# The dense products of layer 3 of a four-layer transformer moved behind the routed experts

## The chip, the cores and the metric

The kernel runs on one core of a Trainium2 chip. The core has a matrix engine (TensorE; its matmuls are PE in the profile, its weight loads PEld), a vector engine (VectorE, DVE), a scalar engine (ScalarE, ACT), a general engine (GpSimd, POOL) and a queue engine that issues plain DMAs (SyncE, SP). Each engine works through its own list of instructions, and engines wait for each other by semaphores. The metric is the device time of one execution in microseconds; the number given is the median of several runs.

## The reference

Four layers work on `x`, 4 rows of 1024 tokens with 128 features. Each layer is a token mixer and a feed-forward part, and after each of the two comes `x = layernorm(x + f(x))`. The change touches the feed-forward part of the last layer, a mixture of experts with a dense "shared" part beside it:

```python
logits = flat.astype(jnp.float32) @ router_w.T + router_bias
scores = jax.nn.softmax(logits, axis=-1)
topk_scores, topk_idx = jax.lax.top_k(scores, TOPK)          # 4 of 32 experts
topk_scores = topk_scores / jnp.clip(topk_scores.sum(axis=-1, keepdims=True), 1e-12, None)
h = jax.nn.silu(jnp.einsum('nd,ehd->neh', flat, gate_w)) * jnp.einsum('nd,ehd->neh', flat, up_w)
expert_out = jnp.einsum('neh,edh->ned', h, down_w)
sel = jnp.take_along_axis(expert_out, topk_idx[:, :, None], axis=1)
out = (sel * topk_scores.astype(flat.dtype)[:, :, None]).sum(axis=1)
out = out + jax.nn.silu(flat @ sgate_w.T) * (flat @ sup_w.T) @ sdown_w.T
```

The last line is the shared part: 128 features up to 512, a gate, and down again, for every token. All sums are in float32.

## The kernel before

`x` stays on the chip as 32 tiles of 128 tokens; a turned copy `xT` feeds the products. For layer 3 the tokens are cut by position into three parts: `a` (the first half of each row, 16 tiles), `b` and `c` (a quarter each, 8 tiles). For each part the work is a chain.

- `l3_attn` (L1621) is the mixer: a norm (BATCH_NORM on VectorE, `rstd` on ScalarE), `sq`, turned into `xq`, products `s`, on VectorE the `y` and `u` chain (L1694 to L1700), products back, a norm, and the turned `xT`.
- `l3_route` (L1718) is the router: softmax, the four largest, and in `positions` a place for each (token, expert) pair in a list sorted by expert. It writes `pos` (L1302).
- `spread` (L1373) scatters the rows of `x` into that list in DRAM (`l3ra`, `l3rb`, `l3rc`) by indirect DMAs that POOL issues, four for a tile: 64 for part a, 32 for b and 32 for c.
- `l3_experts` (`small_experts`, L1781) goes over the list in groups of four tiles: 20 groups for a, 12 each for b and c. For a group, SP loads the rows (`xg`, L1392), PE turns them (`tp`, to `xgT`), multiplies by the gate and up weights (`gu`), ScalarE and VectorE make `sg` and `hg`, PE turns that (`hT`, L173) and multiplies by the down weights (`yp`), ScalarE copies it out (`yg`), and SP writes it to `l3ya`, `l3yb` or `l3yc` (L1830). After the last group `rest_of` (L1414) has a branch (L1418, L1419) over groups that a list has only when it is unusually long.
- `collect` (L1441) gathers each token's four results back (`yt`, again indirect DMAs of POOL, four for a tile, L1327) and adds them to `x` on VectorE with their weights (L1452). The pool of `yt` has eight buffers, taken in turn by all tiles of all parts.
- `finish` (L1866), or `close` (L1946) for part c, norms `x` and writes the output.

The shared part is `l3_shared` (L1749): a block is four tiles. For each of four chunks of 128 hidden features it makes two products of 512 columns (`pg`, `pu`), `sg` on ScalarE and `hs` on VectorE (L764), then 16 products down (`py`). Part a has four blocks, b and c two each.

The order of the work is planned when the program is built. A stage is a main generator and a side generator: `mix(main, side, pace)` runs the main one and, for each unit of planned time that it reports, lets the side report 1/pace units. `press` runs only the side until a condition holds. The side of this stage is called `on`: it holds the mixers and routers of b and c, the scatters of b and c, and the gathers and norms of a and then b. A scheduler then places the instructions on each engine, in an order that is fixed in the built program. What the main generators are, in order:

1. `l3_shared(a)`, then `l3_experts(a)`, at pace 0.45;
2. for b: `l3_shared(b)` as soon as b's mixer is through, its result kept in `sh` by ScalarE copies (L1769), since b's rows are not yet scattered; then `l3_experts(b)`, in whose end (`held`, L1739) `sh` is added to `x`;
3. for c: the same, and `on` is drained inside the end of `l3_experts(c)`;
4. `close(c)`: c's gathers, two tiles for a row, its norm and output.

Of the kernel before, what the change touches and what calls it, by code (L numbers as in the profile page):

```python
# [30 lines left out]
QT = NT // NQT  # L31
# [11 lines left out]
E3, F3, K3 = 32, 128, 4  # L43
# [31 lines left out]
class Kernel:  # L75
# [677 lines left out]

    def glu(self, ps, hp, dst, wg, wu, blk):

        nc = self.nc
        c = slice(blk * BLK, (blk + 1) * BLK)
        pg = self.tile(ps, [P, BLK], "pg")
        self.mm(pg, wg, self.xT[:, c])
        pu = self.tile(ps, [P, BLK], "pu")  # L760
# [3 lines left out]
        nc.vector.tensor_tensor(dst, sg, pu, ALU.mult)  # L764

    def down(self, ps, h, wd, nch):

        py = self.tile(ps, [P, 4, D], "py")
# [969 lines left out]

    def held(self, part, sh):  # L1739

        s = slice(part.t0, part.t0 + part.nt)
        self.nc.vector.tensor_tensor(self.x[:, s, :], sh, self.x[:, s, :], ALU.add)
        yield (1.0,)

    def mark(self, name):
        self.listed.add(name)
        yield (0.0,)

    def l3_shared(self, part, sw, sh=None):  # L1749

        nc, x = self.nc, self.x
        NC = FS3 // P
        with ExitStack() as c2:
            hp = self.pool(c2, "l3sh" + part.name, 2)
            ps = self.pool(c2, "l3sp" + part.name, 2, space=PSUM)
            assert sh is not None or "l3" + part.name in self.listed
            wd = sw[:, 2, :].rearrange("p (c d) -> p c d", d=D)
            for blk in range(part.t0 // 4, (part.t0 + part.nt) // 4):
                h = self.tile(hp, [P, NC, BLK], "hs", bufs=1)
                for c in range(NC):  # L1760
                    f = slice(c * P, (c + 1) * P)
                    self.glu(ps, hp, h[:, c, :], sw[:, 0, f], sw[:, 1, f], blk)
                py = self.down(ps, h, wd, NC)
                if sh is None:
                    s = slice(blk * 4, blk * 4 + 4)
                    nc.vector.tensor_tensor(x[:, s, :], py, x[:, s, :], ALU.add)
                else:
                    t = blk * 4 - part.t0
                    nc.scalar.copy(sh[:, t : t + 4, :], py)  # L1769
                yield (9.0,)  # L1770
# [10 lines left out]
    def small_experts(self, lay, ne, part, wall, held=None):  # L1781

        nc = self.nc
# [3 lines left out]
        with ExitStack() as ctx:  # L1787
# [57 lines left out]
            for g in range(ng + 1):  # L1845
# [7 lines left out]
                if g == ng:  # L1853
                    while held and (got := self.queued(held)):
                        self.now += got[0]
                    self.rest_of(used, tl, total, rest)
                    self.listed.add(f"made {lay}{part.name}")
# [31 lines left out]
    def at_once(self, gen):  # L1889

        for _ in gen:
            yield (0.0,)

    def served(self, gen, *others):
# [46 lines left out]

    def last(self, part, yp):
        yield from self.collect("l3", part, K3, yp)
        yield from self.finish(part)

# [11 lines left out]
    def all(self):  # L1957
# [4 lines left out]
        with ExitStack() as ctx:  # L1962
# [37 lines left out]
            with ExitStack() as c3:  # L2000
                with ExitStack() as c2:
# [12 lines left out]
                    self.abreast(  # L2014
                        self.chain(self.l3_attn(b), self.mark("mixed l3b"), self.l3_route(b)),
                        self.collect("l2", n2, K2, yp, which=(2, 3, 6, 7)),
                    ),
                    self.abreast(
                        self.chain(
                            self.spread("l3", b, K3), self.when(listed("made l3a")), self.last(a, yp),  # L2020
                        ),
                        self.chain(
                            self.l3_attn(c), self.mark("mixed l3c"), self.l3_route(c),
                            self.at_once(self.spread("l3", c, K3)),
                        ),
                    ),
# [12 lines left out]
                self.run(self.close(c, yp))  # L2039
# [183 lines left out]
```

## Time and profile before

| what | value |
|---|---|
| runs (us) | 1927.78, 1932.83, 1929.3; median 1929.3 |
| profiled execution (us) | 1937.33, span 1935.5 |
| PE busy | 1541.5 us, 80% of the span |
| VectorE busy | 1199.2 us, 62% |
| ScalarE busy | 900.6 us, 47% |
| POOL busy | 690.3 us, 36% |
| mean granted PE clock | 0.896 |

The span is the time from the first to the last instruction; the execution is a little longer. The profile gives busy time for each engine, 40 slices of the span with the busy tenths in each, groups of like instructions with what ended the idle time before them, and the instructions in order of time. A share over the whole span says little here: the change touches only the last fifth, from 1549.7 us on, so the stages there are read one by one.

In the last fifth, part a's shared products run from 1549.7 to 1596, its experts to 1708, part b's shared products (with quarter c's routing beside them) to 1743, b's experts to 1793.5, part c's shared products to 1816, c's experts to 1866.5, and the closing work to 1935.5.

### The profile page before, as it was taken

How to read it: one execution, taken by the hardware profiler on the slowest of the kernel's cores; microseconds unless marked ns; L12 is line 12 of the kernel's file. 1: busy time of each engine (PE TensorE's matmuls, PEld its weight loads, DVE VectorE, ACT ScalarE, POOL GpSimd, SP SyncE). 2: the span in 40 equal slices, each digit the busy share in tenths (PEclk: the TensorE clock that was granted, in tenths of full speed). 3: DMA queues.
4: the chain of work that ended last, by engine and by line, in shares of the span. 5: the costliest groups of instructions: out<-in, count | busy, mean ns of one | idle time of the engine just before them, and what ended most of it. 6: DMA issues, size and time to landing. Idle time of an engine off the chain costs nothing. (4 is left out here: it accounts for less than half of the span.)

```text
span 1935.5 us, 27095 instructions
## 1 busy us (share of the span) xinstructions
PE 1541.5 (80%) x9025; PEld 920.8 (48%) x9025; DVE 1199.2 (62%) x3491; ACT 900.6 (47%) x1349; POOL 690.3 (36%) x670
## 2 busy tenths in 40 slices
PE   7885677597847887989977878798798998999850
PEld 3332433385423345856632232333355757768650
DVE  8998698465766664635564565546442446866383
ACT  5876265243324554423336756564532236644330
POOL 2000148604630660265443000030536430567775
PEclk9897688798978998999988988898988999989985
DMA  9990002244430113632241000000452213425452
GB/s 297 288 288 10 1 17 86 87 126 133 159 129 18 60 63 129 183 96 73 78 137 32 1 1 1 2 23 1 159 213 83 66 28 93 141 68 167 122 147 61
DMA packets 215530, 187.10 MB, mean 97 GB/s; under 512 B 16528, under 2 KB 194064, under 8 KB 214864
## 3 DMA queue, kind: packets, MB, share of 16 engines
q1 hardware_dynamic: 194672, 142.29, 23.6%
q0 software_dynamic: 20704, 42.86, 7.3%
q8 instruction: 84, 1.38, 0.3%
q14 instruction: 70, 0.57, 0.1%
HBM read 88.49 MB, written 96.60 MB: 96 GB/s over the span
## 5 line engine op out<-in xcount | busy, mean ns | idle before, releaser
L1081 ACT ACTIVATE pr<-sc 128x1024 f32<-128x1024 f32 x288 | 279.4, 1021 | 175.2 <-PE sc L161 174.8
L161 PE MATMUL sc<-qm,kT 32*128 32x512 f32 (+3 forms) x1536 | 197.7, 559 | 16.7 <-ACT pr L1081 16.7
L161 PE MATMUL s<-pr,va 128*32 128x512 f32 (+3 forms) x1536 | 167.5, 532 | 19.0 <-DVE x L1019 10.2
L161 PE MATMUL gu<-ld,xgT 128*128 x640 | 165.1, 400 | 10.2 <-DVE hg L1812 5.9
L1087 DVE TENSOR_TENSOR pr<-pr,ld 128x512 f32<-128x512 f32 (+1 forms) x160 | 91.7, 581 | 105.6 <-ACT pr L1081 105.4
L161 PE MATMUL gu<-wall,xgT 128*128 x304 | 148.2, 612 | 2.0 <-ACT xgT L171 2.0
L161 PEld LDWEIGHTS sc<-qm,kT 32*128 32x128 f32 x1536 | 83.7, 194 | 112.4 <-issue 61.1
L161 PEld LDWEIGHTS gu<-ld,xgT 128*128 128x128 f32 x640 | 119.5, 198 | 34.7 <-DVE hg L1812 6.1
L1812 DVE TENSOR_TENSOR hg<-sg,gu 128x256 f32<-128x256 f32 x160 | 66.0, 417 | 92.0 <-ACT sg L1811 91.6
L173 DVE COPY hT<-tp 128x512 f32<-128x512 f32 x118 | 80.9, 686 | 66.2 <-PE tp L169 66.2
L1567 ACT ACTIVATE sg<-gu 128x512 f32<-128x512 f32 x76 | 45.4, 597 | 144.7 <-PE gu L161 143.6
L1811 ACT ACTIVATE sg<-gu 128x256 f32<-128x256 f32 x160 | 61.3, 385 | 107.7 <-PE gu L161 79.8
L171 ACT COPY xgT<-tp 128x512 f32<-128x512 f32 x99 | 58.0, 586 | 99.9 <-PE tp L169 99.8
L1327 POOL DMA_INDIRECT l1ra<-x,posl1a x64 | 79.8, 1246 | 61.3 <-DVE peq L1321 42.0
L1327 POOL DMA_INDIRECT l1rr<-x,posl1r x64 | 65.4, 1022 | 100.9 <-DVE posl1r L1302 70.8
L169 PEld LDWEIGHTS tp<-ld,hg 128*128 128x128 f32 x624 | 77.4, 141 | 49.0 <-issue 32.5
L1569 DVE TENSOR_TENSOR hg<-sg,gu 128x512 f32<-128x512 f32 x76 | 51.8, 682 | 78.9 <-ACT sg L1567 78.8
L1327 POOL DMA_INDIRECT l2rm<-x,posl2m x16 | 15.7, 983 | 236.8 <-DVE peq L1320 230.1
L169 PE MATMUL tp<-ld,hg 128*128 128x128 f32 x624 | 96.4, 275 | 3.7 <-DVE hg L1812 2.0
L1327 POOL DMA_INDIRECT l3ra<-x,posl3a x64 | 63.7, 996 | 93.3 <-DVE usedl3a L1315 51.0
L161 PEld LDWEIGHTS s<-pr,va 128*32 128x32 f32 x1536 | 37.1, 113 | 122.6 <-issue 78.4
L161 PE MATMUL yp<-ld,hT 128*128 x640 | 86.1, 276 | 2.3 <-DVE mv L197 1.5
(447 smaller groups left out, 3439.1 us busy)
## 6 DMA issues: line engine op xcount, KB each, us to landing
wall<-wall SPq DMA_DIRECT2D x16, 768.0 KB, 7.8
l3ra<-zero SPq DMA_DIRECT2D x1, 6144.0 KB, 25.5
ld<-in_l_w SPq DMA_DIRECT2D x2, 3072.0 KB, 10.6
wall<-we SPq DMA_DIRECT2D x24, 256.0 KB, 2.1
ld<-in_l_w SPq DMA_DIRECT2D x1, 6144.0 KB, 20.6
l1ra<-zero SPq DMA_DIRECT2D x1, 5120.0 KB, 19.6
l1rr<-zero SPq DMA_DIRECT2D x1, 5120.0 KB, 23.1
xg<-l3ra SPq DMA_DIRECT2D x20, 256.0 KB, 2.9
```

The source lines that it names most:

```text
L161: return self.nc.tensor.matmul(out, lhsT, rhs, start=start, stop=stop)
L169: nc.tensor.transpose(pt[:, k * P : (k + 1) * P], s, self.ident)
L171: nc.scalar.copy(dst, pt[:, : n * P])
L173: nc.vector.tensor_copy(dst, pt[:, : n * P])
L1081: nc.scalar.activation(pr, sc[h], AF.Exp)
L1087: nc.vector.tensor_tensor(d, d, cst["tril"].unsqueeze(1).unsqueeze(1).to_broadcast([P, 2, n, P]), ALU.mult)
L1327: ins = self.nc.gpsimd.indirect_dma_start(**kw)
L1567: nc.scalar.activation(sg, gu[:, 0, :], AF.Silu)
L1569: nc.vector.tensor_tensor(h, sg, gu[:, 1, :], ALU.mult)
L1811: nc.scalar.activation(sg, pg[:, :, 0, :], AF.Silu)
L1812: nc.vector.tensor_tensor(h[:, 2 * c : 2 * c + 2, :], sg, pg[:, :, 1, :], ALU.mult)
```

## The change

Part a's experts come first, and its shared products behind them. Parts b and c then run only their experts. Their shared products, b's two blocks and c's two, come behind the last groups of c's experts, within the same pools of PSUM and ahead of the branch of `rest_of`; what is left of `on` is drained beside them. No result is held back in `sh`: every block is added to `x` at once from PSUM by VectorE, since all rows have been scattered by then. The norms of a and b wait (in the plan) until their shared products are in. The mixer and router of b count 0.6 of their planned time, so that more of them is planned beside the same main work.

```diff
-    def l3_shared(self, part, sw, sh=None):
+    def l3_shared(self, part, sw, ps=None):
...
-            ps = self.pool(c2, "l3sp" + part.name, 2, space=PSUM)
-            assert sh is not None or "l3" + part.name in self.listed
+            ps = ps or self.pool(c2, "l3sp" + part.name, 2, space=PSUM)
+            assert "l3" + part.name in self.listed
...
-                    self.glu(ps, hp, h[:, c, :], sw[:, 0, f], sw[:, 1, f], blk)
-                py = self.down(ps, h, wd, NC)
-                if sh is None:
-                    s = slice(blk * 4, blk * 4 + 4)
-                    nc.vector.tensor_tensor(x[:, s, :], py, x[:, s, :], ALU.add)
-                else:
-                    t = blk * 4 - part.t0
-                    nc.scalar.copy(sh[:, t : t + 4, :], py)
+                    self.glu(ps, hp, h[:, c, :], sw[:, 0, f], sw[:, 1, f], blk, ("tp", "gu"))
+                py = self.down(ps, h, wd, NC, "yp")
+                s = slice(blk * 4, blk * 4 + 4)
+                nc.vector.tensor_tensor(x[:, s, :], py, x[:, s, :], ALU.add)
                 yield (9.0,)
...
                 if g == ng:
-                    while held and (got := self.queued(held)):
+                    for got in held(ps) if held else ():
                         self.now += got[0]
                     self.rest_of(used, tl, total, rest)
...
+    def scaled(self, gen, by):
+
+        for got in gen:
+            yield (got[0] * by, *got[1:])
...
-    def last(self, part, yp):
+    def last(self, part, yp, ready=lambda: True):
         yield from self.collect("l3", part, K3, yp)
+        yield from self.when(ready)
         yield from self.finish(part)
...
-                        self.chain(self.l3_attn(b), self.mark("mixed l3b"), self.l3_route(b)),
+                        self.scaled(self.chain(self.l3_attn(b), self.l3_route(b)), 0.6),
...
-                            self.spread("l3", b, K3), self.when(listed("made l3a")), self.last(a, yp),
+                            self.spread("l3", b, K3), self.when(listed("made l3a")), self.last(a, yp, listed("shared l3a")),
...
-                            self.l3_attn(c), self.mark("mixed l3c"), self.l3_route(c),
+                            self.l3_attn(c), self.l3_route(c),
...
-                    self.when(listed("made l3b")), self.last(b, yp),
+                    self.when(listed("made l3b")), self.last(b, yp, listed("shared l3b")),
                 )
-                self.run(self.mix(self.chain(self.l3_shared(a, sw), self.l3_experts(a, wall3)), on, 0.45, False))
-                hold = self.pool(c3, "l3hold", 2)
-                for p in (b, c):
-                    self.press(on, listed("mixed l3" + p.name))
-                    sh = self.tile(hold, [P, QT, D], "sh")
-                    self.run(self.mix(self.l3_shared(p, sw, sh), on, 0.75, False))
-                    self.press(on, listed("l3" + p.name))
-                    self.press(on, listed("mixed l3c"))
-                    ahead = self.chain(self.held(p, sh), on) if p is c else self.held(p, sh)
-                    self.run(self.mix(self.l3_experts(p, wall3, ahead), on, 0.75, False))
+                self.run(self.mix(self.l3_experts(a, wall3), on, 0.45, False))
+                self.run(self.mix(self.chain(self.l3_shared(a, sw), self.mark("shared l3a")), on, 0.45, False))
+                self.press(on, listed("l3b"))
+                self.run(self.mix(self.l3_experts(b, wall3), on, 0.75, False))
+                self.press(on, listed("l3c"))
+                rest = lambda ps: self.mix(
+                    self.chain(self.l3_shared(b, sw, ps), self.mark("shared l3b"), self.l3_shared(c, sw, ps)), on, 0.75
+                )
+                self.run(self.mix(self.l3_experts(c, wall3, rest), on, 0.75, False))
                 self.run(self.close(c, yp))
```

`glu` and `down` take the names of the PSUM tiles to use, so that the shared products of b and c can use the experts' tiles `tp`, `gu` and `yp`.

More of the change, by code (lines that the diff above doesn't have):

```diff
@@ L751, in weigh, with glu @@
         nc.vector.tensor_tensor(w, w, red.unsqueeze(2).to_broadcast([P, nt, ne]), ALU.mult)
-    def glu(self, ps, hp, dst, wg, wu, blk):
+    def glu(self, ps, hp, dst, wg, wu, blk, tags=("pg", "pu")):
         nc = self.nc
         c = slice(blk * BLK, (blk + 1) * BLK)
-        pg = self.tile(ps, [P, BLK], "pg")
+        pg = self.tile(ps, [P, BLK], tags[0])
         self.mm(pg, wg, self.xT[:, c])
-        pu = self.tile(ps, [P, BLK], "pu")
+        pu = self.tile(ps, [P, BLK], tags[1])
         self.mm(pu, wu, self.xT[:, c])
@@ L764, in glu, with down @@
         nc.vector.tensor_tensor(dst, sg, pu, ALU.mult)
-    def down(self, ps, h, wd, nch):
-        py = self.tile(ps, [P, 4, D], "py")
+    def down(self, ps, h, wd, nch, tag="py"):
+        py = self.tile(ps, [P, 4, D], tag)
         for k in range(4):
@@ L1737, in l3_route @@
             yield (10.0,)
[L1739 to L1743, printed above, removed]
     def mark(self, name):
```

## The prediction

> **What bounds the kernel now.** I read the page's 40 slices first, then the busy time by stage, then the instructions in order of time on SP, VectorE (DVE) and GpSimd (POOL) at the seams between stages. The change lies wholly behind 1549.7 us, where layer 2's last experts end. POOL's slices:
>
> ```profile
> POOL 2000148604630660265443000030536430567775
> PEclk9897688798978998999988988898988999989985
> ```
>
> From slice 36 on POOL shows 6 to 7 tenths; in 10 us slices it is 7.56 us of 10 from 1713 to 1920, one indirect DMA every 1.26 us without a hole. So now the tail is POOL's: 64 gathers of list a, 32 scatters of list c, 32 gathers of b, 32 of c are 160 x 1.26 = 202 us, measured 1712.8 to 1921.2. The engines by stage (columns: stretch, its length, then busy us of PE, PEld, DVE, ACT, POOL, and PE's granted clock):
>
> ```profile
> 1549.70:1596.00 46.30, 43.25 (x201) 27.40 (x202) 20.61 (x52) 16.27 (x30) 15.14 (x16) 1.00 0.11 29
> 1596.00:1657.00 61.00, 55.18 (x328) 44.91 (x328) 45.85 (x168) 35.48 (x68) 0.00 (x0) 0.97 0.33 96
> 1657.00:1708.00 51.00, 46.14 (x288) 37.90 (x286) 40.91 (x126) 31.34 (x61) 35.01 (x32) 1.00 0.45 137
> 1708.00:1743.00 35.00, 32.06 (x127) 20.13 (x125) 20.10 (x81) 15.74 (x25) 23.18 (x24) 0.80 0.20 52
> 1743.00:1793.50 50.50, 45.45 (x291) 40.60 (x289) 30.94 (x76) 23.91 (x49) 38.43 (x40) 0.97 0.57 168
> 1793.50:1816.00 22.50, 21.62 (x96) 13.24 (x96) 5.41 (x8) 5.60 (x10) 17.10 (x18) 1.00 0.27 73
> 1816.00:1866.50 50.50, 45.41 (x288) 40.53 (x288) 27.99 (x73) 23.67 (x49) 37.01 (x39) 0.97 0.63 167
> 1866.50:1877.60 11.10, 0.00 (x0) 0.00 (x0) 10.96 (x55) 1.88 (x3) 7.62 (x9) 0.68 0.58 151
> ```
>
> These are: shared a; experts a up to list b's positions; the rest of experts a; shared b with quarter c's routing; experts b; shared c; experts c; then VectorE alone. PE is busy 289 of 317 us up to 1866.5: barely less full than POOL. The two chains end within 11 us of each other, so whichever the change lengthens decides. Their meeting point:
>
> ```profile
> 1875.33 0.98 POOL L1327 DMA_INDIRECT yt<-l3yb,posl3b  x1 [0.30 <-issue]
> 1877.59 3.44 POOL L1327 DMA_INDIRECT yt<-l3yc,posl3c  x1 [1.28 <-DVE x L1452]
> ```
>
> The first gather of c waited for VectorE's adds of b (L1452), because gathers use eight buffers in turn: c's first tile takes the buffer of b's first. From that gather to the end of the span it is 1935.5 - 1877.6 = 57.9 us, 32 gathers at POOL's pace, the last adds, norm and write: the same in both kernels.
>
> **The change, part by part.** The work is the same but for small things: four ScalarE copies of `sh` (0.59 us each) and two VectorE adds (1.22 us) go, two more block adds of 0.69 us come; no DMA is added, and POOL's order of gathers and scatters stays. Each costs nothing on the path by itself. The extra condition in `last` emits no instruction. What counts is the order, taken from the built program's instruction streams, into which I put the durations of the rows.
>
> (1) Experts a now start the stage, with nothing beside their start. SP may not load their rows until the branch is passed, which waits for the last writes to land. Rows (start us, length, engine, line, operation; in brackets the idle time ahead and what ended it):
>
> ```profile
> 1743.12 15.13 SPq L1392 DMA_DIRECT2D xg<-l3rb  x7
> ...
> 1754.24 0.68 DVE L173 COPY hT<-tp 128x512 f32<-128x512 f32 x1
> ...
> 1761.33 0.68 DVE L173 COPY hT<-tp 128x512 f32<-128x512 f32 x1
> 1764.87 0.68 DVE L173 COPY hT<-tp 128x512 f32<-128x512 f32 x1
> ...
> 1797.68 1.28 DVE L764 TENSOR_TENSOR hs<-sg,pu 128x512 f32<-128x512 f32 x2 [5.18 <-SPq L1419]
> ```
>
> SP released VectorE 4.0 us after the last `l3yb` write was issued (1793.7). The last layer 2 write is issued at 1549.4, so the first load goes out at about 1553. From first load to first `hT` done it is 1754.9 - 1743.1 = 11.8 us, then 1764.87 - 1761.33 = 3.55 us a group. The order puts quarter b's norm behind the fifth `hT`: 1553 + 11.8 + 14.2 = 1579, with its adds 1580. Before, it began at 1584.0: 4 us gained for 42 us of products moved out of the way.
>
> (2) Quarter b's chain, norm to list positions, took 1656.6 - 1584.0 = 72.6 us beside nine groups; now also nine, without four shared products on VectorE (4 x 0.69): 69.5, so 1649.5. From there to the end of experts a it took 51.4 us; five groups fewer remain (5 x 3.55 = 17.8), but quarter c's chain is the same and VectorE, busy 40.9 of 51, gets denser: I add 3. End of experts a: 1686, 22 us earlier. Bounds of (1) and (2): 1675 (loads at 1550, no loss by density) to 1695.
>
> (3) Shared a behind them: four blocks at 10.44 us (their block adds L1766 come at 1561.2, 1571.7, 1582.1) and 1.2 to start, 43 us. Quarter c's norm and routing now run inside. Before, they cost 35 - 22 = 13 us beyond two blocks, part of it at half clock (0.80 mean). By the new order block 2's products wait for the norm and both `xT` copies. I take 12, nearest that row; bounds 4 and 14. End 1741.
>
> (4) Experts b: 50.5 us as before, 1791.5. Then experts c directly: no shared product stands between, so the 4 us of SP's branch, which shared c used to cover, is bare, and so is their start. 1791.5 + 4.3 + 50.5 = 1846. Bounds of the 4.3: 0 and 5.2.
>
> (5) Shared b and c: four blocks, 42 us, to 1888 if undisturbed. But VectorE's order has, ahead of block 3's products, eight adds of the last two tiles of a (2.8 us) and both norms of half a, which before ran in the stretch 1866.5 to 1877.6 with PE idle anyway: 32 statistics (about 7 us), two scalings of eight (2.16 each). In a strict order these are 14 us ahead of block 3's second and third product, of which some 3 are covered by PE's two buffers: 11 us. Bounds 3 (nearly all hidden) and 14; a gain is excluded, since these instructions now only stand ahead of products. End of shared c's last add: 1899.
>
> (6) In VectorE's order all 32 adds of b stand behind that last add. After four of them (1.4) and 1.3 us, as in the row of 1877.59, c's first gather goes at 1902, against 1877.6. Sum +24. The queue behind this wait on POOL is all of c's 32 gathers, and behind them the output.
>
> The Trainium skill, "TensorE: Matmul & The Clock Gate" (section on the array's architecture, engine queue depths), calls VectorE's and ScalarE's queues strict FIFOs. The trace agrees as far as it goes: the add at 1867.86 and the norms came before any add of b, though b's tiles had landed. By the rule the sum stays at +24; if VectorE could pass over the waiting shared products, c's gathers would start when POOL is free, and the sum would be -18.
>
> The same page (Part 1) has PE fall to half clock after about 3.4 us idle and return after as long at work. Here the clock is 0.50 from 1748 to 1751 after 3.4 us idle, inside the 11.8 us used above; but from 1711 to 1723 it stayed at 0.50 with PE at work, longer than the page says, so a measured ramp is used instead of the rule.
>
> The profiled execution took 1937.33 us, 1.8 around its span, and 8.0 above the median 1929.3 of the runs. The sum is a difference inside it; I apply it to the median: 1929.3 + 24 = 1953.
>
> **Rivals.** (a) POOL still sets the end, faster. Positions of b come at 1649.5, its scatters take 44.5 us (measured 1657.5 to 1702.0), and list a is written at 1686 + 3: a's gathers start at about 1695 instead of 1712.8, -18: 1911. For it: POOL has no holes before. Against it: c's first gather needs VectorE through shared c by 1871, and my sum is 28 us past that. That one point decides.
> (b) The seams fill: shared a costs 4 beyond its blocks, the norms cost 3, the bare branch 0: 8 + 8 + 4.3 less, +4, 1933. For it: PE's products need few of VectorE's instructions in shared b and c. Against: each low bound must hold at once.
> (c) PE cools in the new holes, at 1549, 1792 and in block 3, as it did from 1711 to 1723 for 12 us at half clock (6 us lost): twice that, +36, 1965.
>
> **How the numbers follow.** The main case 0.80, (a) 0.06, (b) 0.06, (c) 0.08. A measurement here tells about 0.3%, 6 us, from no change; (a) is faster; (b) lies within it, as does little of the main case; (c) and the rest are slower: 0.06, 0.07, 0.87. Low bounds of (1) to (5) together take off 11 + 8 + 4 + 8, which reaches no change, high ones add 15; a part of each gives 1935 to 1967.
>
> **What would show it.** Right: first load of a's rows at 1552 to 1554; experts a over at 1680 to 1692; a hole of 7 us or more on PE between experts b and c; a's norms within shared c's first block with PE waiting for VectorE; POOL idle for 15 us or more ahead of c's first gather, released by VectorE; PE's last product past 1885. Wrong: POOL without a hole to the end, or shared c's last add before 1875. What would break it most easily is step (2): VectorE packs the chain closer than the rows show, and everything after it moves up.

## The result, and the profile after

The changed kernel took 1935.28 us (median of 20 runs, 1928.87 to 1941.33); the kernel before took 1929.87 us beside it (20 runs). The ratio is 1.0023, 95% interval 1.0012 to 1.0034: slower by 0.23%, some 4 us (the medians differ by 5.4), which is inside the 0.3% that the text had set as no change. The prediction was 1953.0 us, slower by 24; it gave 0.07 to "same". The direction was right and the size was wrong by a factor of five. The time lies 0.3 us inside the low end of the range, which says little for the working: experts a ended earlier than the low bound of steps (1) and (2) allows, as shown below. Some chips run every kernel here about 17% longer (2245 to 2274 us for the kernel before); runs from those are named, and only their ratios to the kernel before on the same chip and the order of their events are read.

Both kernels are the same up to the issue of layer 2's last write, and that instant drifts: it stood at 1549.4 us in the profiled execution before, at 1541.0 in the one after, and between 1540.5 and 1548.0 in the seven other kernels that ran at this speed. So from here on times are counted from it, written with a plus sign: before, the span ends at 1935.5 - 1549.4 = +386.1; after, at 1933.4 - 1541.0 = +392.4. The stretch that the change touches grew by 6.3 us, though the profiled span after is the shorter one.

POOL's 40 slices of the kernel after (48.3 us each):

```profile
POOL 2000147514630660265443000031536321777545
```

POOL is at 7 tenths earlier than before, in slices 35 to 37 (1643 to 1788 us), and then falls to 5 and 4 where the kernel before stood at 7. The engines by stage, as for the kernel before (columns: stretch, its length, busy us of PE, PEld, DVE, ACT, POOL, then PE's granted clock):

```profile
1541.04:1666.50 125.46, 108.35 (x612) 87.98 (x612) 90.21 (x303) 71.43 (x140) 42.34 (x42) 0.93 0.38 111
1666.50:1715.30 48.80, 47.97 (x231) 31.18 (x231) 31.65 (x118) 19.08 (x32) 37.22 (x39) 1.00 0.20 53
1715.30:1765.35 50.05, 46.12 (x288) 41.46 (x288) 29.18 (x72) 22.68 (x47) 38.15 (x40) 0.93 0.54 167
1765.35:1821.45 56.10, 46.41 (x292) 41.46 (x292) 23.80 (x56) 23.85 (x49) 38.04 (x41) 0.91 0.60 162
1821.45:1871.03 49.58, 44.69 (x190) 27.35 (x189) 24.97 (x83) 13.99 (x21) 16.09 (x18) 0.93 0.22 57
```

These are experts a; shared a with route c inside; experts b; the bare branch and experts c; shared b and c. The first stretch is cut at the branch behind experts a; the last product of experts a ends at 1662.74, and quarter c's own products follow up to the branch. Shared a is the surprise: 48.0 of 48.8 us busy, at full clock, although most of quarter c's routing stands in it. The rows that answer to those of the prediction, from the instructions in order of time (start, length, engine, line, operation; in brackets the idle time ahead and what ended it):

```profile
1541.62 15.90 SPq L1392 DMA_DIRECT2D xg<-l3ra  x7
1545.21 1.09 PE L169 MATMUL tp<-ld,xg 128*128 128x128 f32 x4 [4.92 <-DMA xg<-l3ra]
1630.73 0.15 DVE L1302 TENSOR_SCALAR posl3b<-pm 128x32 uint32<-128x32 f32 x1
1774.21 2.29 PE L169 MATMUL tp<-ld,xg 128*128 128x128 f32 x8 [8.86 <-DMA xg<-l3rc]
1850.01 1.70 PE L161 MATMUL gu<-xT,ld 128*128 128x512 f32 x2 [3.39 <-DVE hs L764]
1870.34 0.69 DVE L1759 TENSOR_TENSOR x<-yp,x 128x512 f32<-128x512 f32 x1 [3.26 <-PE yp L161]
1873.37 7.11 POOL L1327 DMA_INDIRECT yt<-l3yc,posl3c  x1 [18.51 <-DVE x L1452]
```

What the reader is to see: list b's positions come at +89.7 (before +107.2); PE idles 8.9 us at the branch behind experts b; it waits for VectorE inside shared c's first block; and POOL stands 18.5 us until VectorE has shared c's last add (1870.34) and the first adds of b behind it. So the place that the prediction named is where the end is decided. Only, it comes 20 us earlier than predicted: c's first gather goes at +332.3, where the text had 1902 - 1549.4 = +352.6, and the kernel before +328.2.

### The profile page after: what moved, and what is told of

Read it like the earlier page. It is cut to its first block, busy times and chain, and to the rows that moved or that the text cites. A ratio compares the mean times of both kernels' runs of the same rounds, so it can differ in the third digit from the quotient of the medians.

```text
span 1933.4 us, 27089 instructions
## 1 busy us (share of the span) xinstructions
PE 1538.2 (80%) x9025; PEld 924.7 (48%) x9025; DVE 1198.5 (62%) x3493; ACT 897.1 (46%) x1346; POOL 692.1 (36%) x670
## 5 line engine op out<-in xcount | busy, mean ns | idle before, releaser
L161 PE MATMUL gu<-ld,xgT 128*128 x640 | 168.6, 407 | 11.2 <-ACT rms L1657 4.4
L1327 POOL DMA_INDIRECT l1ra<-x,posl1a x64 | 79.5, 1242 | 60.1 <-DVE peq L1321 40.9
L169 PE MATMUL tp<-ld,xg 128*128 128x128 f32 x396 | 67.6, 298 | 34.6 <-DMA xg<-l3rc 8.9
## 6 DMA issues: line engine op xcount, KB each, us to landing
ld<-in_l_w SPq DMA_DIRECT2D x1, 6144.0 KB, 19.1
l1ra<-zero SPq DMA_DIRECT2D x1, 5120.0 KB, 19.6
```

The costliest lines, as they stand in the source:

```text
L161: return self.nc.tensor.matmul(out, lhsT, rhs, start=start, stop=stop)
L169: nc.tensor.transpose(pt[:, k * P : (k + 1) * P], s, self.ident)
L1327: ins = self.nc.gpsimd.indirect_dma_start(**kw)
```

## The experiments

Each kernel was timed against the kernel before on the same chip. Unless it is said otherwise the chip is one of two on which the kernel before takes 1931 us. Eleven runs come from four of the slower chips; what they show stands with each kernel and at the end of this section.

**Each part alone.** Which part brings list b forward, and which part costs?

a_only, from the kernel before:

```diff
-                self.run(self.mix(self.chain(self.l3_shared(a, sw), self.l3_experts(a, wall3)), on, 0.45, False))
+                self.run(self.mix(
+                    self.chain(self.l3_experts(a, wall3), self.l3_shared(a, sw), self.mark("shared l3a")), on, 0.45, False
+                ))
...
-                            self.spread("l3", b, K3), self.when(listed("made l3a")), self.last(a, yp),
+                            self.spread("l3", b, K3), self.when(listed("made l3a")), self.last(a, yp, listed("shared l3a")),
```

> Only shared a is moved behind its own experts (with the norms of half a held until it is done); shared b, shared c and their held adds stand as before, and the steps that lead to list b keep their weights. Times are counted from the issue of layer 2's last write (1549.4 in the kernel before, 1541.0 in the changed one): there list b's positions came at +107 and +90, the first gather of c at +328 and +332. Theory (the last block of shared a stood wholly inside the steps to list b, 12 us of them): positions at +88 to +92 although nothing is weighed anew; PE ends its last experts at about +313, since its work is the same; 13 adds of b stand ahead of the last branch, so c's first gather goes at about +317 and the whole is 1917 to 1923 us. Rival 1 (the new weight 0.6 packed the steps): positions at +97 to +100, c's first gather still near +317. Rival 2 (moving shared a is what costs): c's first gather later than +330, 1933 us or more.

Measured: 1944.27 us, ratio 1.0062 (1.0040 to 1.0084). Rows of its instructions in order of time; layer 2's last write was issued at 1541.5:

```profile
1643.50 0.16 DVE L1302 TENSOR_SCALAR posl3b<-pm 128x32 uint32<-128x32 f32 x1
1748.88 0.94 POOL L1327 DMA_INDIRECT yt<-l3ya,posl3a  x1 [16.80 <-DVE x L1452]
1886.63 2.96 POOL L1327 DMA_INDIRECT yt<-l3yc,posl3c  x1 [7.74 <-DVE x L1452]
```

The theory fell on both counts. Positions of b came at +102.0, not +90; and the time got worse, not better. Rival 2 held; rival 1's +97 to +100 was missed by 2 us. POOL, after its first 32 gathers of a, waits 16.8 us for a buffer: a's first adds stand in VectorE's order behind shared a, shared b and route c, which now all come ahead of experts b. c's first gather goes at +345.2.

bc_only, from the changed kernel (and the weight 0.6 taken out as in no_scale):

```diff
-                self.run(self.mix(self.l3_experts(a, wall3), on, 0.45, False))
-                self.run(self.mix(self.chain(self.l3_shared(a, sw), self.mark("shared l3a")), on, 0.45, False))
+                self.run(self.mix(
+                    self.chain(self.l3_shared(a, sw), self.mark("shared l3a"), self.l3_experts(a, wall3)), on, 0.45, False
+                ))
```

> Only shared b and c are moved behind the last experts; shared a stays in front of its experts, and the steps to list b keep their weights. Theory: positions of b at +107 as before; experts b start at about +168 with the routing of c beside them, two bare branches of 8 to 9 us of PE idle, last add of shared c at about +328, c's first gather 2 us behind it at about +331, whole 1931 to 1937 us. Rival (the b and c move alone is what costs, and moving a pays for part of it): c's first gather at +340 or later, 1942 us or more.

Measured: 1968.73 us, ratio 1.0185 (1.0163 to 1.0208). PE and POOL in order of time; the last write was at 1544.2:

```profile
1750.03 3.75 PE L161 MATMUL gu<-ld,xgT 128*128 x8 [20.46 <-DVE pend L1286]
1801.17 1.94 PE L169 MATMUL tp<-ld,xg 128*128 128x128 f32 x8 [17.30 <-DMA xg<-l3rc]
1862.32 0.94 POOL L1327 DMA_INDIRECT yt<-l3yb,posl3b  x1 [25.64 <-DVE x L1452]
```

The theory's 1931 to 1937 us was missed by 32. The rival held, and by more than it said: quarter c's routing now stands beside experts b with no dense products to fill PE (20.5 us idle), its scatters come late (17.3 us more), and POOL stands 25.6 us for b's buffers. c's first gather goes at +369.

**The weight.** no_scale, from the changed kernel:

```diff
-                        self.scaled(self.chain(self.l3_attn(b), self.l3_route(b)), 0.6),
+                        self.chain(self.l3_attn(b), self.l3_route(b)),
```

> The changed kernel without the weight 0.6 on the steps to list b. Theory (the shared block was what stood inside the steps, the weight does little): positions of b at +88 to +93. Rival (the weight packed them): +97 to +100. In this order the norms of half a stand behind shared c's last add and not inside its first block, so that block should lose its 4 us hole, and c's first gather should wait for the norms in its place: 1935 to 1941 us by the theory, 3 to 8 more by the rival.

Measured: 1969.60 us, ratio 1.0190 (1.0167 to 1.0212). Its rows, the last write at 1548.0:

```profile
1650.04 0.16 DVE L1302 TENSOR_SCALAR posl3b<-pm 128x32 uint32<-128x32 f32 x1
1751.92 0.94 POOL L1327 DMA_INDIRECT yt<-l3ya,posl3a  x1 [17.59 <-DVE x L1452]
1807.19 1.97 PE L169 MATMUL tp<-ld,xg 128*128 128x128 f32 x8 [22.66 <-DMA xg<-l3rc]
1877.87 0.95 POOL L1327 DMA_INDIRECT yt<-l3yb,posl3b  x1 [34.96 <-DVE x L1452]
```

By the two ratios that is some 32 us from one number. Positions of b come at +102.1, past the +97 to +100 of the rival and far from the theory's +88 to +93: the weight does pack the steps. The times on record, 1949 us at most, were missed by 20. In the built order thirteen groups of experts a stand between quarter b's norm and list b; with the weight there are nine. And what follows is later too: list c's positions at +197.5 in place of +169.2, so that they miss the place where shared a runs; POOL's hole for a's buffers; experts c waiting 22.7 us for list c's rows; and 35 us for b's.

before_scaled puts the same weight alone into the kernel before:

```diff
-                        self.chain(self.l3_attn(b), self.mark("mixed l3b"), self.l3_route(b)),
+                        self.scaled(self.chain(self.l3_attn(b), self.mark("mixed l3b"), self.l3_route(b)), 0.6),
```

> The kernel before with nothing but the weight 0.6 on the steps to list b. Theory (the weight is what brings list b forward, 12 of the 17 us): positions of b at +94 to +97 in place of +107; POOL bounds the kernel before, so it gains what POOL starts earlier, 1915 to 1922 us. Rival (adds of a stand later in VectorE's order and hold POOL's gathers by their buffers, as in the kernel with shared a alone moved): a hole of 10 us or more on POOL ahead of a's ninth tile and 1930 us or more.

Its first run is from a slower chip; before_scaled_2 is the same kernel.

> The kernel of before_scaled again: the kernel before with the weight 0.6 alone. Theory (POOL bounds that kernel and starts 12 us earlier): positions of b at +94 to +97 in place of +107, 1915 to 1922 us. Rival (POOL's order changes with the weight: list c's scatters now stand ahead of all of a's gathers, and adds of a hold buffers in experts b): a hole of 10 us or more on POOL or PE, and 1930 us or more.

Measured in the second run: 1934.03 us, ratio 1.0026 (1.0011 to 1.0042). The last write was at 1540.7:

```profile
1637.25 0.15 DVE L1302 TENSOR_SCALAR posl3b<-pm 128x32 uint32<-128x32 f32 x1
1707.71 0.16 DVE L1302 TENSOR_SCALAR posl3c<-pm 128x32 uint32<-128x32 f32 x1
1708.61 0.95 POOL L1327 DMA_INDIRECT l3rc<-x,posl3c  x1 [25.34 <-ACT yg L1826]
```

The weight does what the theory said of the list (+96.6 in place of +107.2), and the rival held on the time. List c's positions come early enough that its 32 scatters stand ahead of all 64 gathers of a in POOL's order, so POOL, done with list b at 1683, stands 25.3 us. The profile names a ScalarE copy as what ended that wait, but the scatter needs list c's positions and goes 0.7 us behind them. The start is earlier and the gain is handed back. So none of the three parts is good alone: weight +0.26%, shared a's move +0.62%, the move of b and c +1.85%, both moves without the weight +1.90%, all three +0.23%. They are not terms of a sum: each decides which work stands beside which.

**What binds c's first gather.** It waits for a buffer that b's adds free, and POOL also has to pass the branch behind experts c (`rest_of`, L1419). Which of the two binds?

yt16, from the changed kernel:

```diff
-                yp = self.pool(c3, "l3y", 8)
+                yp = self.pool(c3, "l3y", 16)
```

> The changed kernel with 16 buffers for gathered rows in place of 8, so that c's first gather needs no add of b. Theory (c's gathers wait only for b's adds, which stand behind shared c's last add): POOL's holes of 5.5, 7.1, 5.6 and 18.5 us go, c's gathers start before shared c is done, and the end is set by VectorE: last shared add at +330 as now, then 64 adds of 0.27 us, the norms and the write, +360 to +370 in place of +392: 1905 to 1915 us. Rival (the branch behind shared c holds POOL as well): c's first gather at about +331, 1931 to 1936 us.

Measured: 1940.85 us, ratio 1.0043 (1.0023 to 1.0063). PE and POOL, the last write at 1542.6:

```profile
1744.13 3.72 PE L161 MATMUL gu<-ld,xgT 128*128 x8 [19.57 <-DVE hg L1802]
1880.18 0.94 POOL L1327 DMA_INDIRECT yt<-l3yc,posl3c  x1 [42.58 <-SPq L1419]
```

POOL's three holes among b's gathers closed, as the theory said, but c's first gather now waits 42.6 us, ended by SP at the branch, and goes at +337.6. So the branch holds POOL too, as the rival said, and both times on record were missed. But the edit did more than it was meant to: `collect` adds a tile only once all buffers are filled, so a's adds also moved in VectorE's order, and PE lost 19.6 us in experts b behind adds whose rows hadn't come. keep8 takes that away: 16 buffers, and an add follows its gather by at most 8 tiles as before, so that VectorE's order is that of the changed kernel.

```diff
-            if len(late) == yp.bufs:
+            if len(late) == min(yp.bufs, 8):
...
-                yp = self.pool(c3, "l3y", 8)
+                yp = self.pool(c3, "l3y", 16)
```

> The changed kernel with 16 buffers for gathered rows, but an add still follows its gather by at most 8 tiles, so VectorE's order is that of the changed kernel to the instruction; only the buffers differ. Theory (c's first gather waits for a buffer that b's adds free, and these stand behind shared c's last add): POOL's holes of 5.5, 7.1 and 5.6 us close, b's gathers end near +297 from layer 2's last write, and c's first gather goes when SP has issued half a's output and passed the last branch, near +317 in place of +332; the end moves by as much, 1913 to 1921 us. Rival (the branch releases POOL only when shared c is done on PE and VectorE): c's first gather at +330 or later and no gain, 1931 to 1937 us.

The first run is from a slower chip; keep8_2 is the same kernel.

> The kernel of keep8 again: on the chip of its first run even the kernel before took 2273.6 us, with PE idle up to 27 us at a time behind no releaser, so those times answer nothing. Theory as before (a buffer binds c's first gather): first gather near +317 from layer 2's last write in place of +332, 1913 to 1921 us where the kernel before takes 1930. Rival (the branch releases POOL only when SP has issued half a's output, and this comes late): +325 or later, 1925 us or more.

Measured in the second run: 1919.57 us, ratio 0.9947 (0.9929 to 0.9964), as the theory had it. The last write was at 1541.5; SP (the output of half a), POOL and VectorE in order of time:

```profile
1848.06 4.67 SPq L1863 DMA_DIRECT2D out_x<-x  x8
1855.12 0.94 POOL L1327 DMA_INDIRECT yt<-l3yc,posl3c  x1 [19.11 <-SPq L1419]
1868.19 8.71 DVE L1452 SCALAR_TENSOR_TENSOR x<-yt,wkl3b,x 128x128 f32<-128x128 f32 x32
1871.46 6.26 POOL L1327 DMA_INDIRECT yt<-l3yc,posl3c  x1 [0.30 <-issue]
```

c's first gather goes at +313.6, 12.5 us ahead of shared c's last add (1867.58) and not behind it. Both kernels issue VectorE's work in the same order; only the buffers differ. So the buffer bound the changed kernel, and with it gone the branch binds, 18.7 us earlier. early_keep8 also moves that branch, from behind shared c to between shared b and shared c, and plans c's gathers beside shared c:

```diff
-                    self.chain(self.l3_shared(b, sw, ps), self.mark("shared l3b"), self.l3_shared(c, sw, ps)), on, 0.75
+                    self.chain(self.l3_shared(b, sw, ps), self.mark("shared l3b")), on, 0.75, False
...
-                self.run(self.close(c, yp))
+                on = self.chain(on, self.close(c, yp, listed("shared l3c")))
+                self.run(self.mix(self.chain(self.l3_shared(c, sw), self.mark("shared l3c")), on, 0.75))
```

> Both edits: the last branch between shared b and shared c, and 16 buffers. Theory: neither wait is left, c's first gather goes near +305, POOL is done near +346, and the end is VectorE's: shared c's last add at about +330, 64 adds of 0.27 us, norms and write behind it, +360 to +368 in place of +392: 1903 to 1912 us. Rival (GpSimd's gathers slow VectorE or PE down by running beside shared c): last add of shared c later than +336, and 1915 us or more.

> The kernel of early_keep8 again, for the same reason. Theory: the last branch between shared b and shared c and 16 buffers leave neither wait; c's first gather near +305, the end is VectorE's, +360 to +368 in place of +392, 1903 to 1912 us where the kernel before takes 1930. Rival: the norms and output of half a, now behind that branch, move nothing and the gain is that of 16 buffers alone, within 3 us of the other run.

Measured in the second run: 1899.11 us, ratio 0.9834 (0.9812 to 0.9856), the fastest of all, ahead of both kernels and of the theory's 1903 to 1912. The last write was at 1540.5:

```profile
1773.85 1.94 PE L169 MATMUL tp<-ld,xg 128*128 128x128 f32 x8 [9.10 <-DMA xg<-l3rc]
1836.09 0.95 POOL L1327 DMA_INDIRECT yt<-l3yc,posl3c  x1 [0.30 <-issue]
1868.25 8.48 DVE L1452 SCALAR_TENSOR_TENSOR x<-yt,wkl3b,x 128x128 f32<-128x128 f32 x32
```

c's gathers follow b's without a hole, from +295.6 where the theory had +305, and the end is now VectorE's: 64 adds and the norms behind shared c's last add (1867.64). Both rivals are out: shared c's last add stands at +327.1, no later than in the changed kernel (+330.0), and the gain is 20 us more than that of the buffers alone.

if_c_early has the moved branch with 8 buffers.

> The changed kernel with the last branch (the rest of list c's tiles) between shared b and shared c, where it stood behind shared c, and 8 buffers as it is. Theory (the buffer is what binds): c's first gather stays near +332, 2 us behind shared c's last add, and the time is that of the changed kernel, 1931 to 1939 us. Rival (the branch binds): c's first gather near +315 and 1915 to 1922 us.

All three runs of it (if_c_early, if_c_early_2, if_c_early_3) are from slower chips.

> The kernel of if_c_early again: the changed kernel with the last branch between shared b and shared c and 8 buffers; its first run was on a chip where all kernels took 17% longer. Theory (the buffer binds first, the branch only after it): c's first gather stays near +332, 2 us behind shared c's last add, ratio to the kernel before 1.000 to 1.004, that of the changed kernel. Rival (the branch alone is worth something): c's first gather at +325 or earlier and a ratio of 0.997 or less.

> The kernel of if_c_early a third time. Theory (the buffer binds first): c's first gather 2 us behind shared c's last add, near +332, ratio 1.000 to 1.004. Rival (the branch alone is worth something): +325 or earlier, 0.997 or less.

Ratios there: 0.9963 (0.9909 to 1.0017), 1.0005 (0.9967 to 1.0044), 1.0017 (0.9979 to 1.0056). The first lies where the rival had it, but its interval holds 1; the other two are the theory's: no gain is shown. The order of events can still be read; the first run's rows:

```profile
2222.80 0.69 DVE L1759 TENSOR_TENSOR x<-yp,x 128x512 f32<-128x512 f32 x1 [3.26 <-PE yp L161]
2225.60 2.38 POOL L1327 DMA_INDIRECT yt<-l3yc,posl3c  x1 [17.16 <-DVE x L1452]
```

With the branch out of the way the gather still goes 2.1 us behind shared c's last add (2222.80 + 0.69), released by VectorE's adds, and it is 2.1 us in the other two runs as well. That, and keep8_2, answer the question from both sides: the buffer binds first, the branch behind it.

**The idle time ahead of experts c.** split_b is early_keep8 with one block of shared b put ahead of the branch behind experts b:

```diff
-                self.run(self.mix(self.l3_experts(b, wall3), on, 0.75, False))
+                one = lambda ps: self.mix(self.l3_shared(b, sw, ps, slice(0, 1)), on, 0.75, False)
+                self.run(self.mix(self.l3_experts(b, wall3, one), on, 0.75, False))
...
-                    self.chain(self.l3_shared(b, sw, ps), self.mark("shared l3b")), on, 0.75, False
+                    self.chain(self.l3_shared(b, sw, ps, slice(1, 2)), self.mark("shared l3b")), on, 0.75, False
```

> early_keep8 with shared b's first block ahead of the branch behind experts b, so that PE has 10.4 us of work while SP passes it. Theory (the 9.1 us of PE idle there is the bare branch and nothing else): the hole shrinks to 3 to 4 us, experts c start about 5 us later and end so, one block fewer follows them, and shared c's last add comes 5 to 6 us earlier, near +321 from layer 2's last write; the end is VectorE's behind that add, so 1892 to 1896 us where the kernel before takes 1930, ratio 0.980 to 0.982. Rival (list c's rows or POOL's gathers, not the branch, hold the start of experts c): the hole stays at 8 us or more, and the time within 2 us of early_keep8, ratio 0.983 to 0.985.

> The kernel of split_b again: on the chip of its first run the kernel before took 2244.9 us, so that its times don't answer the question. Theory (the 9.1 us of PE idle behind experts b is the bare branch): the hole shrinks to 3 to 4 us, shared c's last add near +321 from layer 2's last write, 1892 to 1896 us where the kernel before takes 1930, ratio 0.980 to 0.982. Rival (rows or gathers hold the start of experts c): a hole of 8 us or more, ratio 0.983 to 0.985.

> The kernel of split_b a third time, if the chip is one on which the kernel before takes 1930 us. Theory (the 9.1 us of PE idle behind experts b is the bare branch): the hole shrinks to 3 to 4 us, shared c's last add near +321 from layer 2's last write, ratio to the kernel before 0.980 to 0.982. Rival (rows or gathers hold the start of experts c): a hole of 8 us or more, ratio 0.983 to 0.985.

All on slower chips: ratios 1.0120 (1.0072 to 1.0168), 1.0060 (1.0017 to 1.0103), 1.0070 (1.0015 to 1.0125), neither the theory's nor the rival's. The hole was 5.4, 7.4 and 7.5 us in the three runs, between the two numbers, where early_keep8 on such a chip has 6.7: it didn't shrink as the theory had it. The rival's reason is out too: in the second run list c's scatters were done at 2023, 97 us before the first load. From that run, SP and PE:

```profile
2112.88 3.17 PE L161 MATMUL yp<-ld,hs 128*128 128x128 f32 x26 [0.18 <-DVE hs L764]
2120.27 6.66 SPq L1392 DMA_DIRECT2D xg<-l3rc  x4
2123.47 1.94 PE L169 MATMUL tp<-ld,xg 128*128 128x128 f32 x8 [7.43 <-DMA xg<-l3rc]
```

The first load goes 4.2 us behind the end of the block, as it goes 3.9 us behind the last product of experts b in early_keep8's first run, and 1770.7 - 1765.35 = 5.4 us behind it in the changed kernel at the usual speed. SP's wait of 11.2 us ahead of this load is ended by PE at the branch. So work ahead of the branch moves the branch with it and covers nothing; in the kernel before, shared c stood behind the branch, and the load went 0.03 us after its last product. The experiment was aimed wrong, and a block behind the branch wasn't tried.

**The weight with the other place of shared a.** bc_scaled is bc_only with the weight 0.6 kept.

> The changed kernel with shared a in front of its experts again, the weight 0.6 kept: of the three parts only shared a's move is undone. Theory (the weight is worth its 33 us only together with shared a's move, because otherwise list c's scatters come ahead of all of a's gathers and adds of a hold experts b): positions of b at +94 to +97, a hole of 15 us or more on PE inside experts b, c's first gather behind shared c and half a's norms, 1955 to 1975 us. Rival (the weight brings its gain with either place of shared a): no such hole, 1935 to 1942 us.

> The kernel of bc_scaled a second time. Theory (the weight and shared a's move act only together): list c's scatters ahead of all of a's gathers, a hole of 15 us or more on PE or POOL inside experts b, 1955 to 1975 us. Rival (the weight brings its gain with either place of shared a): 1935 to 1942 us.

Both on slower chips: 1.0042 (1.0006 to 1.0079) and 0.9991 (0.9925 to 1.0056). In both POOL does have list c's scatters ahead of all of a's gathers, as before_scaled_2 shows it at the usual speed. PE stands 39 us inside experts b in both, but on these chips kernels without that order show holes of 27 and 37 us there too (below), so that sign decides nothing; what the order costs at the usual speed stays open.

**The slower chips.** Beside the kernel before there, keep8 was slower, 1.0126 (1.0038 to 1.0214), early_keep8 not told from no change, 1.0041 (0.9989 to 1.0093), and before_scaled 1.0050 (0.9997 to 1.0103). So the gains of keep8 and early_keep8 are shown for one chip and not for those. Two rows of keep8's first run, PE inside experts b:

```profile
2001.85 3.78 PE L161 MATMUL gu<-ld,xgT 128*128 x8 [26.66 <-issue]
2045.95 3.42 PE L161 MATMUL gu<-ld,xgT 128*128 x8 [37.38 <-ACT xgT L171]
```

In that stage PE has 49.9 us of records in 126 us, where keep8_2 has 44.9 in 55, with as many matmuls (288); the idle time lies ahead of the expert groups' products, with no releaser, or with one that is itself late behind nothing the trace shows. ScalarE and VectorE stand some 10 us at a time in the same stretch, while POOL's gathers between the two rows go on every 1.25 us up to 2038. The rows tell where the time goes and not why. No cause was found.

## Why the prediction was wrong, by its own steps

In the profiled executions, counted from layer 2's last write (the prediction's times minus 1549.4), with "experts a over" at the last product of their last group, the mark of the text's 1708:

| step | predicted | measured | difference |
|---|---|---|---|
| (1) quarter b's norm begins | +30.6 | +28.4 | -2.2 |
| (2) list b's positions | +100.1 | +89.7 | -10.4 |
| (2) experts a over | +136.6 | +121.7 | -14.9 |
| (3) shared a over | +191.6 | +174.3 | -17.3 |
| (4) experts b over | +242.1 | +224.3 | -17.8 |
| (4) experts c over | +296.6 | +280.4 | -16.2 |
| (5) shared c's last add | +349.6 | +330.0 | -19.6 |
| (6) c's first gather | +352.6 | +332.3 | -20.3 |
| end of the span | +410.1 | +392.4 | -17.7 |

The chain of waits was right, and the place where it is decided; step (2) made the size wrong, 13 of the 20 us.

Step (2), 8 us in the chain to list b: this is the step that failed. The text took the kernel before's 72.6 us from norm to positions, saw nine groups of experts in both orders, and took off 4 x 0.69 us for the shared products that no longer stand there. But in the kernel before, 12 of those 72.6 us (1584 to 1596) are shared a's last block, on PE, with no group at all; its nine groups lie in the other 60.6. From the kernel before, on VectorE: the norm's first instruction, the add of the last block, and the first group:

```profile
1584.02 0.29 DVE L196 BATCH_NORM_STATS2 bn<-x 128x6 f32<-128x128 f32 x1
1596.14 0.69 DVE L1766 TENSOR_TENSOR x<-py,x 128x512 f32<-128x512 f32 x1 [0.29 <-PE py L161]
1608.12 0.69 DVE L173 COPY hT<-tp 128x512 f32<-128x512 f32 x1
```

The changed kernel has nine groups and no block: 89.7 - 28.4 = 61.3 us. The cost of the block was taken from VectorE's list when PE's was the one that held it. The other kernels agree, each from its own trace:

| kernel | groups between norm and positions | shared block there | us |
|---|---|---|---|
| before | 9 | yes | 72.6 |
| before_scaled_2 | 5 | yes | 61.9 |
| after | 9 | no | 61.3 |
| no_scale | 13 | no | 73.2 |
| a_only | 13 | no | 74.8 |

The block is worth 11 us, and four groups 11 to 14. The nine groups that the text counted in the new order were the work of the weight 0.6, which it didn't name: without it four more groups stand where the block was, and the chain is 73 us again. So the weight is what turns the room into time, 12 of the 17.5 us that list b came forward. The text named step (2) as what would break most easily, though for another reason: VectorE packing the chain closer.

Step (2), 4.5 us more from positions to the end of experts a: 32.0 us where the text had 36.6. The 3 us that it added for a denser VectorE were not there. The low bound of (1) and (2), 1675, was +125.6; the measured +121.7 lies below it.

Step (3), 2.4 us: from the last product of experts a to that of shared a it took 1715.3 - 1662.7 = 52.6 us, 9.6 above the four blocks' 43, where the text had 12 from a stage at mean clock 0.80. In the changed kernel this stage has clock 1.00, and PE is busy 50.3 of the 52.5 us.

Step (5), 3 us: the 11 us of stall by half a's norms were right in place and too large. Shared c's first block took from 1843.06 to 1861.86, 18.8 us, where a block takes 10.44: 8.4. The eight adds, the statistics and the two scalings took 10.7 us of VectorE there and not 14: the statistics, put at 7, took 4.2. PE's idle time in the block is 3.4 and 0.6 us, with the clock at 0.53 from 1850 to 1857.

Step (1), 2 us: SP's wait for the last write's landing wasn't there. The first load was issued 0.6 us behind that write, not 3.6: in the trace of the changed kernel SP passes that branch at 1534.9 to 1535.2, ahead of the write and not behind it. From the load to the end of the first `hT` it took 12.1 us, where the row had given 11.8.

Step (4) went the other way for experts c, by 1.3 us: the first load went 5.4 us behind the last product of experts b, where the text had 4.3. PE stood 8.9 us in all.

Step (6) held: VectorE's order puts all of b behind shared c, and the ninth tile's buffer makes POOL wait for it, 2.3 us behind the last add. keep8_2 confirms it by taking it away. The text took the path from that gather to the end as unchanged at 57.9 us; it was 60.1: the first gather took 7.11 us and not 3.44, and the third 0.94 where it had taken 2.06 (below).

Of the rivals, (b), the seams fill, gave 1933 and is near in size by luck. It had shared a's overhead at 4 (9.6 measured), the norms at 3 (8.4) and the branch at 0 (5.4 ahead of the load): none came about. Most of the difference came from step (2), which it did not touch. Rival (a) failed by its own condition: the point of decision was shared c's last add by 1871 - 1549.4 = +322, and it came at +330. Rival (c) didn't happen: the stages' mean clock is 0.91 to 1.00 throughout. The text's "without a hole" for POOL in the kernel before is nearly so: there are holes of 1.75 us ahead of b's first gather and 1.28 ahead of c's.

The Trainium skill, "TensorE: Matmul & The Clock Gate" (engine queue depths), calls VectorE's queue a strict FIFO; nothing here speaks against it: all 32 adds of b start right after shared c's last add (1870.95 after 1870.34), though b's last gather had been issued at 1853.9.

## What to carry to other kernels

When a chain of steps is spread between groups of other work, its length is counted from the engine that is full there, block by block; what is moved away frees that engine's time and not the small share that another engine had in it. A weight in a planner is a term of the change like any other: build both orders, with and without it, and count what stands between the same two marks. And before a move is blamed or praised, look for the one buffer that ties an early transfer to late work: on top of three reorderings that together brought nothing, eight more buffers and the last branch moved ahead of shared c brought 1.7% on one chip. Whether those two edits would help the kernel before, without the reorderings, was not tried; c's first gather waits only 1.3 us there.

## What the runs showed of the hardware

While VectorE runs its 32 adds of b without a pause, a gather on POOL can last until that run is over. Three kernels show it, with the gather at different places in the run: after, the run ends at 1870.95 + 8.71 = 1879.66 and the gather at 1873.37 + 7.11 = 1880.48; keep8_2, 1876.90 and 1877.72; early_keep8_2, 1876.73 and 1871.29 + 6.25 = 1877.54. The gather ends 0.8 us behind the run each time, where its neighbours take 0.94 in all. Not every gather in a run is held to its end. In keep8_2 the two ahead of the held one, begun in the run's first 2 us, took 0.98 and 1.00. In the kernel before, 30 adds run from 1875.93 to 1883.93: c's first gather there took 3.44 us and ended inside the run, at 1881.03, the second took 1.06, and the third was held to 1884.75, again 0.8 behind:

```profile
1882.69 2.06 POOL L1327 DMA_INDIRECT yt<-l3yc,posl3c  x1 [0.30 <-DMA yt<-l3yc,posl3c]
```

The Trainium skill, "SBUF — State Buffer" (who interferes with whom), has VectorE and GpSimd share a port pair under an exclusive lock, and says of a tensor_tensor with both inputs in SBUF that it contends with GpSimd's reads and, as an inference, does not stall the making of descriptors. The adds here are of another kind, scalar_tensor_tensor, and what lets one gather of a run pass and holds another isn't shown; that the port is the reason wasn't tried.

The branch behind a list's tiles holds the engines in two ways that cost differently. Behind experts b, where no product stands between it and experts c, and list c's rows are ready, SP's first load comes 5.4 to 5.9 us after PE's last product in the four kernels that show it at the usual speed (after, yt16, keep8_2, early_keep8_2), and 2.5 to 6.1 on the slower chips. PE's own branch instruction (L1419) takes 4.3 us there in the kernel after and 3.5 to 3.8 in the other three, where it takes 0.34 in the kernel before; it ends at 1769.7 in the kernel after, SP's last semaphore of the branch comes at 1770.3, and the load at 1770.7. Why PE's instruction takes that long is not shown. And POOL goes on, by the profile, when SP has passed: in keep8_2 SP first issues half a's output, from 1848.06 to 1852.73, which waits for half a's norms, and POOL goes on at 1855.12. So POOL stands 19.1 us at a branch with which it has nothing to do.
